# Layer a's reciprocals of the sums of weights: held in the buffer of their spread copies instead of the buffer of the FFN's normalized row

## The chip, the cores and the metric

The kernel runs on one core of one Trainium2 chip. The metric is the time of one execution on the device in microseconds (us), as the median of three runs. One more execution was taken with the hardware profiler, and all durations below come from that one.

## The reference, cut to what matters

The input `x` has 4 sequences of 2048 rows of 512 values in fp32. Four layers follow each other, each on a layer norm of the running `x` and each added to it: a linear attention with 16 heads of 64 (layer a), an FFN in int8, a gated recurrence (layer b), and the same FFN again. The change lies in layer a and its FFN:

```python
q = relu(q) + EPS;  k = relu(k) + EPS
k_cumsum = cumsum(k, axis=2)
context  = cumsum(einsum('bhnd,bhne->bhnde', k, v), axis=2)
D_inv = 1.0 / einsum('bhnd,bhnd->bhn', k_cumsum, q)      # reciprocal of the sum of weights
attn  = einsum('bhnd,bhnde,bhn->bhne', q, context, D_inv)
x = x + attn @ Wo + bo
# FFN: each row of layernorm(x) is divided by its largest magnitude / 127, rounded, and multiplied
x = x + ffn(layernorm(x), rhs)
```

## The kernel before, in words

**Tiles and stages.** The program has two bodies; the one that these inputs take is `layer_a_mild` followed by `layer_b_mild`. Layer a cuts the 8192 rows into 16 blocks of 512 (`n` = 0 to 15, four for each sequence) and the 16 heads into 8 pairs (`hp` = 0 to 7). For each block the loop goes over the pairs. I call one turn of it a pair step. In a pair step, `attend(B, hp)` gives the attention work of that pair in six parts (`keys`, `scores`, `update`, `weigh`, `outputs`, and an empty one), and `spread` puts the filler matmuls between them. The filler is: the keys and queries of the next pair (`feature`), a piece of the values (`values`), and the tail of the block before: in steps 0 to 3 the output projection of one row tile of 128 rows (`project`, tile `po`, line 648), in steps 4 to 7 the FFN product of one row tile (`pf`, line 681).

**One pair step, by engine.** TensorE forms `pk` and `pq`; VectorE turns them into `kT` and `qT` (line 804). A copy of `kT` is split into 16-bit `planes` (line 710), turned by a DMA transpose (line 712) and joined by ScalarE into `kr` (line 717). TensorE forms the scores `pss` (line 888), VectorE masks them into `sm` (line 894), one for each head. TensorE forms the updates `pu`, ScalarE copies them to `u` (line 909), and GpSimd adds them into `within` in three dependent rounds of two additions (line 914): the state in front of each of the four chunks. Then TensorE forms the outputs `pn` from these states (line 968) and from `sm` (line 974), ScalarE copies them to `oT` (line 983), and GpSimd makes the last addition into `state` (line 979). VectorE keeps running sums of the keys in `qc` (lines 869, 872, 876).

**The weights, every fourth pair.** In steps 3 and 7, `weigh` sums the weights of four pairs in `pd` (line 926). ScalarE takes the logarithm into `f_y` (line 931) and the exponential of its negative into `guess` (line 933), each with a table load ahead of it; VectorE improves this reciprocal by one Newton step (lines 935 and 936); a DMA stores eight rows of it to `rec` in DRAM (line 938), and pairs of DMAs read it back with each row copied over 64 partitions into `wide` (line 959), two pairs of heads at a time. `divide` multiplies `oT` by `wide` (line 950) in the pair step that follows. The tile `guess` carries the name `f_xn`.

**The FFN of the block before.** `levels(prev, i)` is written after pair steps 3 to 6 for row tiles 0 to 3: statistics (lines 124 to 127; 126 and 127 run on GpSimd), the normalized row in `f_xn` (line 131), its largest magnitude (664 to 666), the scaled and rounded row (668, 670) in `f_q`, and a DMA transpose into `f_qT` (line 676). In block 0 the same buffer `f_xn` also takes the four parts of the FFN's weight while they are quantized (line 691).

**What sets the order.** Tiles are named buffers of a pool; tiles with the same name share its `bufs` slots, and `f_xn`, `f_y` and `wide` have one slot each. A scheduler fixes the order of the instructions on each engine when the program is built, from the order of the code, the dependencies, and the moment at which a slot comes free. At run time every engine works its own list strictly in order. PSUM tiles of the tag `mm` (`pk`, `pq`, `pv`, `po`, `pf`, `pd`) share three banks in rotation.

Of the kernel before, what the change touches and what calls it, by code (L numbers as in the profile page):

```python
# [10 lines left out]
F32 = mybir.dt.float32  # L11
# [8 lines left out]
P = 128  # L20
# [9 lines left out]
TA = 512  # L30
# [16 lines left out]
def hybrid_block_kernel(ctx: ExitStack, tc: tile.TileContext, t: dict, out: bass.AP):  # L47
# [674 lines left out]
    def layer_a_mild():  # L722
        with ExitStack() as es:
            w = es.enter_context(tc.tile_pool(name="ma_w", bufs=1))
            pool = es.enter_context(tc.tile_pool(name="ma", bufs=2))
# [123 lines left out]
            def attend(B, hp):  # L849
# [69 lines left out]
                def weigh():  # L919


                    if hp % 4 != 3:
                        return
                    pd = bank([P, TA], F32, name="pd", tag="mm")
                    for m in range(4):
                        nc.tensor.matmul(
                            pd[m * 32 : (m + 1) * 32, :], same, B.qc[hp - 3 + m],
                            start=True, stop=True, skip_group_check=True,
                        )
                    ln = pool.tile([P, TA], F32, name="f_y", bufs=1)  # L930
                    nc.scalar.activation(ln, pd, AF.Ln)
                    guess = pool.tile([P, TA], F32, name="f_xn", bufs=1)
                    nc.scalar.activation(guess, ln, AF.Exp, scale=-1.0)

                    nc.vector.scalar_tensor_tensor(ln, pd, -1.0, guess, ALU.mult, ALU.mult)
                    nc.vector.scalar_tensor_tensor(guess, ln, 2.0, guess, ALU.add, ALU.mult)
                    rec = dram.tile([4, 2, TA], F32, name=f"rec_{B.n}_{hp}")
                    nc.sync.dma_start(rec.rearrange("m h t -> (m h) t"), guess[0:P:16, :])

                    if B.n + 1 == len(at) and hp == NP - 1:  # L940
                        wide = pool.tile([P, 4, TA], F32, name="xnTa")
                        for h, r in enumerate(heads):
                            nc.sync.dma_start(wide[r, :, :], rec[:, h, :].partition_broadcast(DA))
                        wides = [wide[:, 0:2, :], wide[:, 2:4, :]]
                    else:
                        wides = [load(rec, 0)]

                    def divide(m):
                        o = B.oT[hp - 3 + m]
                        nc.vector.tensor_tensor(o, o, wides[m // 2][:, m % 2, :], ALU.mult)  # L950
                        if m == 1 and len(wides) == 1:
                            wides.append(load(rec, 2))

                    weights.extend([lambda m=m: divide(m) for m in range(4)])

                def load(rec, m):
                    wide = pool.tile([P, 2, TA], F32, name="wide", bufs=1)
                    for h, r in enumerate(heads):
                        nc.sync.dma_start(wide[r, :, :], rec[m : m + 2, h, :].partition_broadcast(DA))
                    return wide  # L960

                def outputs():
# [20 lines left out]
                    nc.scalar.copy(B.oT[hp], pn.rearrange("p i t -> p (i t)"))  # L983

                return [keys, scores, update, weigh, outputs, lambda: None]

            def block(n, x):
# [574 lines left out]
```

## Time and profile before

| | |
|---|---|
| median of three runs | 4108.96 us (4106.58 to 4109.81) |
| profiled execution: its own time / its span | 4114.83 / 4113.0 us |
| TensorE busy | 3992.1 us, 97% of the span |
| VectorE / GpSimd / ScalarE busy | 57% / 36% / 21% of the span |
| mean granted TensorE clock | 0.989 |
| layer a | from 0 to about 2480 us; an inner block takes about 151 us |
| one pair step of an inner block | about 21.4 us in steps 0 to 2, about 15.4 us in steps 5 and 6 |

The profile was read in one execution. A wait of an engine is the idle time ahead of an instruction, put down to what ended it. Matmuls are pipelined and their ends are modelled, so a TensorE that looks busy may still not be at its peak; its idle stretches, on the other hand, are real.

### The profile page before, as it was taken

Reading aid. Unit: us, or ns where it says so; the run is one execution under the profiler, and the core shown is the slowest. Engines: PE = TensorE matmul, PEld = TensorE weight load, DVE = VectorE, ACT = ScalarE, POOL = GpSimd, SP = SyncE. Lnnn points to the kernel's source line nnn. Section 1 sums busy time; section 2 is a strip of 40 time slices with the busy share of each in tenths; the row PEclk is TensorE's granted clock in tenths of the full one; section 3 lists DMA queues with packets and bytes.
Section 4 is the critical chain, followed back from the end, with each engine's and each line's share of the span. In section 5 each row is a group of like instructions: output and inputs, shape, how many; then the busy total and the mean of one; then the engine's idle time right before and its main releaser. Section 6 shows DMA issues by size and latency. Waiting matters only on the chain.

```text
span 4113.0 us, 54684 instructions
## 1 busy us (share of the span) xinstructions
PE 3992.1 (97%) x21333; PEld 2203.9 (54%) x21333; DVE 2363.5 (57%) x4575; ACT 884.0 (21%) x1420; POOL 1492.9 (36%) x2527
## 2 busy tenths in 40 slices
PE   8999999999999999999999987999999999999997
PEld 4554554554544554554554544666666666666664
DVE  4455555555555455455455455666666666666665
ACT  2222212222222222222122111222222222222221
POOL 3122322322232323232232223455444554444543
PEclk9999999999999999999999998999999999999998
DMA  4112212212222222221121123121221221211111
GB/s 134 33 38 58 61 37 62 57 39 65 52 42 65 55 53 51 52 67 38 51 68 39 37 51 123 42 52 47 51 48 47 47 48 48 49 49 47 52 32 28
DMA packets 432045, 217.32 MB, mean 53 GB/s; under 512 B 363808, under 2 KB 376992, under 8 KB 431776
## 3 DMA queue, kind: packets, MB, share of 16 engines
q1 hardware_dynamic: 430656, 212.16, 21.3%
q8 instruction: 169, 2.77, 0.3%
q10 hardware_dynamic: 1120, 1.57, 0.1%
q14 instruction: 100, 0.82, 0.1%
HBM read 91.49 MB, written 34.08 MB: 31 GB/s over the span
## 4 chain that ended last, share of the span: by engine, by line
PE 72%; DVE 10%; POOL 10%; DMA 4%; issue 2%; ACT 2%; SPq 0%; POOLq 0%; DVEq 0%; ACTq 0%
PE pk L648 10%; PE pv L648 9%; PE pq L648 9%; PE pr L1215 8%; PE po L648 8%; PE py L648 5%; PE pvb L648 3%; PE pss L888 3%; PE pn L974 3%; PE pn L968 2%; PE pf L681 2%; DVE st L124 2%; PE ps L1308 2%; POOL rs L127 2%; PE pl L1248 2%
## 5 line engine op out<-in xcount | busy, mean ns | idle before, releaser
L648 PE MATMUL pq<-xnTa,a_Wq 128*128 128x512 f32 x1024 | 493.6, 610 | 0.0
L648 PE MATMUL pk<-xnTa,a_Wk 128*128 128x512 f32 x1024 | 491.1, 604 | 0.0
L648 PE MATMUL pv<-a_Wv,xnTa 128*128 128x512 f32 x1024 | 477.3, 605 | 2.9 <-ACT xnTa L141 2.9
L648 PE MATMUL po<-a_Wo_sb,oT 128*128 128x512 f32 x1024 | 468.7, 603 | 7.0 <-DVE oT L950 6.9
L914 POOL TENSOR_TENSOR within<-state,u 64x64 f32<-64x64 f32 x256 | 129.9, 507 | 654.7 <-ACT u L909 645.1
L126 POOL TENSOR_SCALAR rs<-mv 128x1 f32<-128x1 f32 x320 | 85.8, 269 | 728.1 <-DVE mv L125 530.7
L648 PEld LDWEIGHTS po<-a_Wo_sb,oT 128*128 128x128 f32 x1024 | 189.7, 191 | 236.7 <-issue 217.7
L648 PEld LDWEIGHTS pv<-a_Wv,xnTa 128*128 128x128 f32 x1024 | 189.5, 192 | 234.8 <-issue 229.9
L909 ACT COPY u<-pu 128x256 f32<-128x256 f32 x128 | 47.6, 372 | 1131.3 <-PE pu L904 1036.3
L648 PEld LDWEIGHTS pq<-xnTa,a_Wq 128*128 128x128 f32 x1024 | 182.2, 190 | 193.6 <-issue 183.3
L648 PEld LDWEIGHTS pk<-xnTa,a_Wk 128*128 128x128 f32 x1024 | 184.8, 190 | 180.6 <-issue 157.7
L894 DVE TENSOR_TENSOR sm<-pss,causal 128x512 f32<-128x512 f32 x256 | 164.7, 685 | 193.0 <-PE pss L888 193.0
L1215 PE MATMUL pr<-xnTb,m_kT_sb 128*128 128x256 f32 x1024 | 259.5, 392 | 0.0
L1215 PE MATMUL pr<-xnTb,m_qT_sb 128*128 128x256 f32 x1024 | 253.4, 391 | 0.0
L648 PE MATMUL pvb<-b_vT_sb,xnTb 128*128 128x512 f32 x512 | 242.7, 607 | 0.0
L648 PE MATMUL py<-b_oT_sb,yT 128*128 128x512 f32 x512 | 231.6, 594 | 0.0
L838 DVE TENSOR_TENSOR xa<-po,xa 128x512 f32<-128x512 f32 x64 | 44.1, 690 | 320.3 <-PE po L648 320.3
L1215 PEld LDWEIGHTS pr<-xnTb,m_qT_sb 128*128 128x128 f32 x1024 | 188.1, 191 | 63.7 <-issue 31.5
L1354 POOL TENSOR_TENSOR state_b<-pairs,m_diag 128x256 f32<-128x256 f32 x128 | 98.4, 769 | 327.9 <-DVE pairs L1332 298.1
L1215 PEld LDWEIGHTS pr<-xnTb,m_kT_sb 128*128 128x128 f32 x1024 | 184.7, 190 | 51.0 <-issue 19.9
L914 POOL TENSOR_TENSOR within<-within,u 64x64 f32<-64x64 f32 x512 | 192.2, 375 | 38.4
L717 ACT COPY kr<-turned 128x1024 uint16<-128x1024 uint16 x120 | 139.3, 1160 | 302.3 <-DMA turned<-planes 302.3
(157 smaller groups left out, 6533.2 us busy)
## 6 DMA issues: line engine op xcount, KB each, us to landing
wide<-rec SPq DMA_DIRECT2D x124, 256.0 KB, 3.6
mmid<-xa SPq DMA_DIRECT2D x16, 1024.0 KB
out<-xb SPq DMA_DIRECT2D x32, 512.0 KB, 2.8
xa<-in_x SPq DMA_DIRECT2D x15, 1024.0 KB
xb<-mmid SPq DMA_DIRECT2D x30, 512.0 KB, 7.4
turned<-planes SPq DMA_TRANSPOSE x304, 3.1
m_cos<-in_cos SPq DMA_DIRECT2D x30, 128.0 KB, 2.4
m_sin<-in_sin SPq DMA_DIRECT2D x30, 128.0 KB
```

Source lines behind the costliest of these rows:

```text
L124: nc.vector.bn_stats(st[:, i, :], x[:, i, :])
L126: nc.gpsimd.tensor_scalar(rs, mv[:, :, 1], LN_EPS, None, ALU.add)
L127: nc.gpsimd.tensor_tensor(rs, rs, neg_half[:, :n], ALU.pow)
L648: nc.tensor.matmul(held[0], lhs(), rhs(), start=(n == 0), stop=(n == len(pairs) - 1))
L681: nc.tensor.matmul(pf, qT[:, c, :], rq[:, c, :], start=(c == 0), stop=(c == KC - 1))
L717: nc.scalar.copy(dst.bitcast(U16).rearrange("p n (t two) -> p n t two", two=2), turned.rearrange("p (two n) t -> p n t two", two=2),)
L888: nc.tensor.matmul(ps[h][:, i, :], k[r, chunks[i]], q[r, chunks[i]], start=True, stop=True)
L894: nc.vector.tensor_tensor(s, ps[h], causal.unsqueeze(1).to_broadcast([P, NTA, P]), ALU.mult)
L914: nc.gpsimd.tensor_tensor(A.before[i + 1][r, r], A.before[i][r, r], u[r, i, :], ALU.add)
L974: nc.tensor.matmul(pn[r, i, :], v()[:, i, vh[h]], A.sm[h][:, i, :], start=False, stop=True, skip_group_check=True,)
L1215: nc.tensor.matmul(pr[:, half, :], wp[name][:, c, lo : lo + P], B.xnT[:, c, :], start=(c == 0), stop=(c == KC - 1),)
L1354: nc.gpsimd.tensor_tensor(st.rearrange("p (q c) -> p q c", c=2 * DB), pairs[:, g, :].unsqueeze(1).to_broadcast([P, HG // 2, 2 * DB]), smal ...
```

## The change

The tile that holds `guess` takes the name `wide` instead of `f_xn`. It is the first half of a tile of the shape that `load` uses, so that it lives in the one slot of `wide`. No arithmetic, no transfer and no buffer is added or removed.

```diff
                     ln = pool.tile([P, TA], F32, name="f_y", bufs=1)
                     nc.scalar.activation(ln, pd, AF.Ln)
-                    guess = pool.tile([P, TA], F32, name="f_xn", bufs=1)
+                    guess = pool.tile([P, 2, TA], F32, name="wide", bufs=1)[:, 0, :]
                     nc.scalar.activation(guess, ln, AF.Exp, scale=-1.0)
 
                     nc.vector.scalar_tensor_tensor(ln, pd, -1.0, guess, ALU.mult, ALU.mult)
                     nc.vector.scalar_tensor_tensor(guess, ln, 2.0, guess, ALU.add, ALU.mult)
                     rec = dram.tile([4, 2, TA], F32, name=f"rec_{B.n}_{hp}")
                     nc.sync.dma_start(rec.rearrange("m h t -> (m h) t"), guess[0:P:16, :])
```

## The prediction

> **What bounds the kernel now.** I first read the busy shares, then what TensorE waits for, then the timeline of one inner block of layer a on all engines.
>
> ```profile
> PE 3992.1 (97%) x21333; PEld 2203.9 (54%) x21333; DVE 2363.5 (57%) x4575; ACT 884.0 (21%) x1420; POOL 1492.9 (36%) x2527
> PE pf L681 <- DMA f_qT<-f_q: 25.4, 5, 9.1
> PE pn L968 <- POOL within L914: 21.1, 25, 1.2
> ```
>
> TensorE sets the end: 97% busy, so only its own idle time can be won, and a VectorE wait costs something only if TensorE later runs dry. Its waits (sum, times, longest) show where. `pf` on `f_qT` falls on the last microseconds of layer a and on layer b, outside the change. The 25 waits on `within` are layer a's. By the timeline 1.82 us of them fall in block 0 and 1.21 in steps 5 and 6 of block 15; the other 18.04 us all stand in pair step 4: in blocks 1 to 14 they are 1.21, 0.81, 2.17, 0.81, 0.83, 0.83, 1.55, 0.90, 0.81, 0.80, 0.83, 0.81, 0.82, 2.13 (sum 15.31), in block 15 0.77 + 0.96 + 1.00 = 2.73. Block 4 stands for the others (start, duration, engine, ...; in brackets the idle time before it):
>
> ```profile
> 706.17 0.63 ACT L933 ACTIVATE f_xn<-f_y 128x512 f32<-128x512 f32 x1
> 710.38 0.55 DVE L131 TENSOR_SCALAR f_xn<-xa,mv,rs 128x512 f32<-128x512 f32 x1 [1.63 <-DMA rec<-f_xn]
> ...
> 719.05 1.28 DVE L894 TENSOR_TENSOR sm<-pss,causal 128x512 f32<-128x512 f32 x2
> ...
> 722.69 1.54 DVE L950 TENSOR_TENSOR oT<-oT,wide 128x512 f32<-128x512 f32 x2
> 724.15 1.34 DVE L869 TENSOR_TENSOR_SCAN qc<-go,kT 128x512 f32<-128x512 f32 x1
> ...
> 721.76 1.19 POOL L914 TENSOR_TENSOR within<-state,u 64x64 f32<-64x64 f32 x2
> 723.02 3.07 POOL L914 TENSOR_TENSOR within<-within,u 64x64 f32<-64x64 f32 x4
> ...
> 726.15 0.49 PE L968 MATMUL pn<-qT,within 128*128 128x128 f32 x2 [0.81 <-POOL within L914]
> ```
>
> VectorE has no gap from 710.38 to 730.2, because all four FFN rows are packed behind the store of `guess`. The last four GpSimd additions take 3.07 us there; in step 0 of the same block they take
>
> ```profile
> 657.14 0.70 POOL L914 TENSOR_TENSOR within<-state,u 64x64 f32<-64x64 f32 x2 [3.69 <-ACT u L909]
> 657.91 1.48 POOL L914 TENSOR_TENSOR within<-within,u 64x64 f32<-64x64 f32 x4
> ```
>
> They are slow while VectorE runs lines 950 and 869, so the third pair of `pn` matmuls starts at 726.15 instead of 725.34.
>
> [...] 3.07 against 1.48 us under lines 950 and 869 (two SBUF inputs each), and in step 5 the first two additions take 1.61 instead of 0.70 under line 869. [...]
>
> **The change, part by part.** The lists of instructions of the changed program, which has not run, show what moves.
>
> (1) Removed: the FFN rows no longer wait for `guess` to be stored. That wait is 27.0 us of VectorE in 15 times, none of it on TensorE: worth 0 by itself.
>
> (2) Added: `guess` waits for the slot of `wide`. The last `divide` is at 724.2 in step 4, the next `guess` at 773.6 in step 7, the one after in the next block: free some 50 us ahead, 0. The other way, `wide` cannot be loaded before `guess` is stored, but the load reads `rec`, so it waits for that store already: 0. Nothing queued on SP sees a new wait from it.
>
> (3) Moved: rows 0, 1 and 2 go on VectorE to steps 0, 1 and 2, right behind line 838 and the statistics, ahead of `sm`; row 3 stays in step 4. GpSimd's lines 126 and 127 for rows 0 to 2 go along, at 0.22 + 0.57 us each, while GpSimd is idle. Two `f_qT` transposes (1.2 us of SP each) go to steps 0 and 1, ahead of that step's `turned`; `f_q` is done just before `planes`, so `kr` slips by at most one transpose more.
>
> What it costs in steps 0 to 2: from the trace of step 4 one row takes 2.67 us (710.38 to 713.05), after 1.05 us for the two GpSimd instructions. In step 2, line 838 starts at 692.31, statistics end at 693.93, the row runs from 694.98 to 697.65, so `sm` comes at 697.65 instead of 695.97 and `planes` 1.7 us later than 697.89. TensorE needs `sm` at 707.6 and the bank of `pk` at 705.7: covered. In steps 0 and 1 `sm` comes 2.5 us later; line 869 then falls on the third round of `within` (658.8 to 660.1), which ends near 660.4 instead of 659.4, while TensorE asks for it at 663.3 in step 0: 2.9 us of cover. So 0.
>
> What it brings in step 4: the later `planes` of step 2 delays `kr`, and on ScalarE `kr` stands ahead of the logarithm.
>
> ```profile
> 701.79 1.16 ACT L717 COPY kr<-turned 128x1024 uint16<-128x1024 uint16 x1 [1.97 <-DMA turned<-planes]
> 702.97 1.28 ACT L931 ACT_TABLE_LOAD   x1
> 782.60 1.29 DVE L950 TENSOR_TENSOR oT<-oT,wide 128x512 f32<-128x512 f32 x2 [3.18 <-DMA wide<-rec]
> ```
>
> So line 936 ends at 708.49 + 1.66 = 710.15. Store and spread take 6.3 us (step 7: line 936 ends at 776.26, line 950 starts at 782.60). VectorE is idle in between, line 950 starts at 716.45, and the list goes on: 838, 950, statistics to 719.13, row 3 starts at 720.2, its line 664 ends at 721.4, `sm` to 722.6, `kT` 723.4, `planes` 724.2. Only then, 724.2 to 726.7, come line 869 and two of line 950. `u` is ready at 721.5; six additions of 0.37 us with their gaps, from 721.76, end near 724.1, ahead of the 725.34 that TensorE needs. I leave 0.1 us a block for chance overlap. In block 15, counted the same way (`u` 0.25 us behind TensorE), 0.25 us remains. The late `qT` (728.7) still frees its bank before 730.3.
>
> Gain: 18.04 - 14 x 0.1 - 0.25 = 16.4 us.
>
> (4) Block 0: `guess` waited for the quantized part in `f_xn` and held ScalarE until 111.9, with `rscale` behind it, for which TensorE waited 0.51 us. That wait goes; two instead of four score matmuls stand ahead of the transpose, so I count 0.3 us.
>
> Sum: -16.7 us. The profiled execution took 4114.83 us, of which 1.83 lie around its span; it becomes 4098.1. The median lies 5.9 us below that execution, so 4108.96 - 16.7 = **4092.3 us**, -0.41%. Unknown: [...] the landing of `wide` in its new surroundings (6.3 us, perhaps 1 either way).
>
> **Rivals.** I take 0.2% of the time, 8.2 us, as what a measurement of this kernel can tell from no change.
>
> A. *The blocked stretch only shifts.* If `kr` is not delayed by all of 1.7 us, line 869 starts near 723.3, and the last two additions are caught behind it and line 950. The wait then stays at 0.7 to 0.8 us in every block: 14 x 0.75 = 10.5 of 15.31 remain, and about 1 us is won in block 15: 4108.96 - 5.8 = 4103 us. For it speaks that only 0.1 to 0.9 us separate the additions' end from line 869; against it, that each step of the delay is a direct wait in the trace.
>
> B. *Slower: `within` becomes late in steps 0 and 1.* Row, `sm`, `kT`, `planes` and 869 now run without a gap just when `within` is due. If the third round is held until line 876 is through as well (662.7), and the row starts later because its statistics stand second on GpSimd, it misses 663.3 by about 0.9 us in both steps: 2 x 15 x 0.9 = 27 us, less 16.7: 4119 us. It decides from 2.9 us of further delay on. The step is 21.4 us long, which speaks against it.
>
> C. *The 27 us of VectorE wait come off the end*: 4082 us. TensorE shows no gap at those times, so hardly.
>
> D. *The change does nothing* (the slot of `wide` is busy, the rows wait as before): 4109 us; the lists already show the rows moved, so only as part of "same".
>
> **How the numbers follow.** My forecast 0.58, A 0.25 (a little of it beyond 8.2 us), B 0.12, C 0.02, D 0.03. Faster by over 0.2%: 0.58 + 0.02 + 0.05 of A = 0.65. Same: 0.20 + 0.03 = 0.23. Slower: 0.12. The forecast's own range is 4088 (all of 21.1 us but block 0's, and some noise) to 4100. For eight in ten it reaches over A: 4086 to 4108.
>
> **What would show it.** Right: the waits of `pn` on `within` fall from 21.1 us to about 4.7; in step 4 the last four additions take about 1.5 us; the wait on `rec` is gone from `f_xn`; `f_xn` rows stand in steps 0 to 2; the exponential of step 3 comes 1.7 us later against TensorE. Wrong: waits of `pn` of 0.7 us still in step 4 (A), new waits in steps 0 and 1 (B), or a new wait of TensorE on `kT`, `qT` or `sm`.

## The result, and the profile after

The changed kernel takes **4083.38 us** (median of four runs, 4082.97 to 4084.23) against 4109.09 us before (4106.58 to 4109.81) in the same comparison: ratio 0.9939, 95% interval 0.9922 to 0.9956. That is 25.7 us less. The prediction said 4092.3 us, with 4086 to 4108 as its range: the direction was right, the gain half as large again as forecast. The profiled execution took 4082.97 us, its span 4081.2 us. Two executions in a slow state, of 8099.94 us (late1) and 5806.78 us (one_input), are left out of the medians given below.

Busy shares, and TensorE's waits (sum, times, longest), of the changed kernel:

```profile
PE 3972.0 (97%) x21211; PEld 2197.0 (54%) x21333; DVE 2356.3 (58%) x4575; ACT 875.9 (21%) x1420; POOL 1506.4 (37%) x2527
```
```profile
PE pf L681 <- DMA f_qT<-f_q: 24.9, 5, 9.1
PE po L648 <- DVE oT L950: 6.1, 2, 5.7
PE pn L968 <- POOL within L914: 4.1, 7, 1.2
```

The busy shares say nothing here (122 matmul records are missing from this trace). The waits do: those of `pn` on `within` went from 21.1 us to 4.1, where 4.7 was forecast. That is 17.0 us, and the kernel became 25.7 us faster. The rest of this text is about that difference.

Timeline of block 4, pair step 4, of the changed kernel, on ScalarE, VectorE, GpSimd and TensorE:

```profile
714.25 0.37 ACT L909 COPY u<-pu 128x256 f32<-128x256 f32 x1 [10.74 <-PE pu L904]
```
```profile
709.58 0.69 DVE L950 TENSOR_TENSOR oT<-oT,wide 128x512 f32<-128x512 f32 x1 [6.23 <-DMA wide<-rec]
...
713.36 0.55 DVE L131 TENSOR_SCALAR f_xn<-xa,mv,rs 128x512 f32<-128x512 f32 x1 [1.07 <-POOL rs L127]
...
716.51 0.69 DVE L710 COPY planes<-kT 128x1024 uint16<-128x1024 uint16 x1
717.12 1.34 DVE L869 TENSOR_TENSOR_SCAN qc<-go,kT 128x512 f32<-128x512 f32 x1
718.39 1.47 DVE L950 TENSOR_TENSOR oT<-oT,wide 128x512 f32<-128x512 f32 x2
```
```profile
714.70 0.70 POOL L914 TENSOR_TENSOR within<-state,u 64x64 f32<-64x64 f32 x2 [1.38 <-ACT u L909]
715.48 1.90 POOL L914 TENSOR_TENSOR within<-within,u 64x64 f32<-64x64 f32 x4
```
```profile
717.84 0.83 PE L968 MATMUL pn<-qT,within 128*128 128x128 f32 x6
```

I measure from the start of the `u` copy (line 909), because TensorE sets it in both kernels. The additions end at 715.48 + 1.90 = 717.38, which is u + 3.13; before it was 723.02 + 3.07 - 721.14 = u + 4.95. Line 869 starts at u + 2.87 and the last two of line 950 behind it, so that they hardly touch the additions (the last four take 1.90 us, against 1.48 in step 0 of block 4 before). All six `pn` matmuls run in one stretch of 0.83 us.

**Where the time came from.** The distance from one `u` copy to the next gives the length of a step without any model of where a matmul ends. From the copy of step 4 to that of step 5, blocks 1 to 14 take 14.51 to 14.57 us now. Before, ten of them took 15.59 to 15.73 us (I call these ten the plain blocks), block 1 16.21, block 7 16.64, block 3 18.76, block 14 18.83; block 15 went from 17.35 to 11.68. The sum over the 15 blocks falls by 28.8 us, of the 31.8 us by which the two spans differ; the waits listed there had been 18.04 us. Outside block 0 the other steps have kept their lengths within 0.1 us, but for the stretch from step 0 to step 1, where 2.2 us of scattered waits are gone.

### The profile page after: what moved, and what is told of

Same layout as the page of the kernel before. It is cut to its first block, busy times and chain, and to the rows that moved or that the text cites. A ratio compares the mean times of both kernels' runs of the same rounds, so it can differ in the third digit from the quotient of the medians.

```text
span 4081.2 us, 54608 instructions
## 1 busy us (share of the span) xinstructions
PE 3972.0 (97%) x21211; PEld 2197.0 (54%) x21333; DVE 2356.3 (58%) x4575; ACT 875.9 (21%) x1420; POOL 1506.4 (37%) x2527
## 4 chain that ended last, share of the span: by engine, by line
PE 83%; POOL 8%; DVE 6%; issue 1%; DMA 1%; ACT 0%; SPq 0%; POOLq 0%; ACTq 0%; DVEq 0%
PE pk L648 11%; PE pv L648 11%; PE pq L648 11%; PE po L648 11%; PE pr L1215 8%; PE py L648 5%; PE pss L888 3%; PE pvb L648 3%; PE pn L974 3%; PE pn L968 3%; PE pf L681 2%; PE pu L904 2%; PE ps L1308 2%; PE pl L1248 2%; PE pg L648 2%; DVE st L124 2%
## 5 line engine op out<-in xcount | busy, mean ns | idle before, releaser
L126 POOL TENSOR_SCALAR rs<-mv 128x1 f32<-128x1 f32 x320 | 70.7, 221 | 765.9 <-DVE mv L125 765.6
L914 POOL TENSOR_TENSOR within<-state,u 64x64 f32<-64x64 f32 x256 | 156.5, 611 | 523.0 <-ACT u L909 513.4
L127 POOL TENSOR_TENSOR rs<-rs,neg_half 128x1 f32<-128x1 f32 x320 | 193.4, 605 | 23.3
```

The costliest lines, as they stand in the source:

```text
L127: nc.gpsimd.tensor_tensor(rs, rs, neg_half[:, :n], ALU.pow)
L914: nc.gpsimd.tensor_tensor(A.before[i + 1][r, r], A.before[i][r, r], u[r, i, :], ALU.add)
```

## The experiments

Two questions: why does step 4 become faster, and why by more than its waits? *Theory M*: VectorE instructions that read two tiles (lines 950 and 869) no longer run on top of GpSimd's additions. *Rival S*: the 27 us that the FFN rows waited for a store were the cost. On the price: a *linear* price (a wait costs its idle time) against *theory P* (more). The answers in short: the wait for the store cost almost nothing by its length, but it set the order of VectorE's work so that lines 950 and 869 fell on the additions; and a wait of TensorE cost more than its idle time, by a lost overlap of matmuls (0.27 us in a plain block) and, where waits piled up, by the clock (0.50 for 3.41 us or more). In the expectations, "the sum of the waits" is that of the profile's list. Each comparison had its own runs of the kernel before, with medians of 4111.3 to 4112.5 us.

### What a wait costs: late1, late2, late4

The changed kernel, with one, two or four useless GpSimd instructions that make `within` late.

```diff
                     nc.scalar.copy(u, pu)
+                    if B.n and hp == 4:
+                        for _ in range(2):      # 1, 2, 4
+                            nc.gpsimd.tensor_scalar(u, u, 1.0, None, ALU.mult)
```

> The changed kernel with two multiplications by 1 of `u` on GpSimd ahead of the additions in step 4 of blocks 1 to 15: `within` comes some 0.8 us later there. It measures what a wait of TensorE costs. In the changed kernel the additions end 0.3 to 0.9 us before TensorE needs them, so a wait of 0 to 0.5 us in each of 15 blocks. Linear price (a wait costs its idle time): lost time = sum of the new waits, 0 to 8 us. Theory P (a wait costs its idle time and about 0.27 us more for the restart of the matmuls, and far more where two waits stand close): 1.3 to 1.6 times the sum of the waits.

> As with two multiplications, but four: `within` some 1.6 us later, waits of 0.7 to 1.5 us in each of 15 blocks, some in two or three pieces. Linear price: lost time = sum of the new waits, 10 to 22 us. Theory P: each wait costs about 0.27 us more than its idle time, and where two or three of them stand within 3 us the granted clock falls behind them and the price is about 2 us for each us of idle time: lost 20 to 40 us, and the intervals between the `u` copies of these steps lengthen by more than the waits listed in them.

> The changed kernel with one multiplication by 1 of `u` on GpSimd ahead of the additions in step 4 of blocks 1 to 15. With two of them the waits were 33 us longer and the time 68 us. Linear price: lost time equals the new waits. Theory P: where one wait stands alone, the step lengthens by its idle time and 0.2 to 0.3 us more, at a full granted clock; where two or three stand within 3 us, by twice the idle time, at a clock of 0.5 to 0.9 over some 4 to 8 us. Waits of 0.3 to 0.8 us, in one piece in most blocks: 4095 to 4105 us.

Medians: 4102.70 us with one, 4151.69 with two, 4194.01 with four; that is 19.3, 68.3 and 110.6 us above the changed kernel. The waits of `pn` (one line each from the profiles of late1, late2 and late4):

```profile
PE pn L970 <- POOL within L916: 18.6, 23, 1.2
```
```profile
PE pn L971 <- POOL within L917: 37.5, 45, 1.4
```
```profile
PE pn L971 <- POOL within L917: 61.4, 49, 4.2
```

Over the 4.1 us of the changed kernel these are 14.5, 33.4 and 57.3 us more. A microsecond of listed wait costs 1.3, 2.0 and 1.9 us. The linear price is refuted. The waits were longer than I had expected (in block 4 a useless instruction takes 0.86 to 1.36 us, at least twice what I had assumed). The price for single waits was as expected in late1, where most blocks have one wait of 1.02 to 1.15 us and a step 1.2 to 1.4 us longer; for piled waits it was the 2 that I had expected of late4, and it was that in late2 already, where I had expected 1.3 to 1.6.

**The first part of the price** is lateness that is not shown as idle. One plain block (block 4) in each kernel, both times measured from its own `u` copy:

| kernel | additions end | wait listed | step longer than 14.57 |
|---|---|---|---|
| changed | 3.13 | 0 | 0 |
| one_input_869 | 3.65 | 0 | 0 |
| kr_pe | 4.03 | 0 | 0.15 |
| one_input | 4.42 | 0.28 | 0.54 |
| before | 4.95 | 0.81 | 1.08 |
| rows_stored | 4.98 | 0.57 | 1.10 |
| late1 | 5.17 | 1.02 | 1.26 |

The last column is the first minus 3.9, within 0.03 us, in all rows where it is above zero. So TensorE is held up from u + 3.9 on, not from u + 4.2 as the prediction took from the waits. Before, four `pn` matmuls took 0.61 us and the last two, behind the wait, 0.49 us; without the wait all six take 0.83. The overlap of matmuls that follow each other was lost at the wait, and that 0.27 us (0.61 + 0.49 - 0.83) appears as busy time. In rows_stored it was lost twice: its first four `pn` matmuls on `within` take 0.88 us, with no wait listed among them.

**The second part** is the clock. TensorE in late2, block 4, and four windows of the same step (us, busy time of PE, PEld, DVE, ACT and POOL, granted TensorE clock, DMA share, GB/s):

```profile
728.16 0.49 PE L971 MATMUL pn<-qT,within 128*128 128x128 f32 x2 [0.56 <-POOL within L917]
729.61 0.49 PE L971 MATMUL pn<-qT,within 128*128 128x128 f32 x2 [0.96 <-POOL within L917]
730.67 0.79 PE L971 MATMUL pn<-qT,within 128*128 128x128 f32 x2 [0.57 <-POOL within L917]
731.39 1.98 PE L977 MATMUL pn<-sm,va 128*64 128x128 f32 x16
```
```profile
723.90:727.90 4.00, 3.70 (x10) 1.59 (x9) 4.00 (x8) 0.32 (x1) 3.35 (x4) 1.00 0.20 67
727.90:731.90 4.00, 2.20 (x12) 1.60 (x14) 3.97 (x10) 1.16 (x1) 3.47 (x7) 0.83 0.34 66
731.90:735.90 4.00, 4.00 (x20) 2.36 (x18) 0.86 (x4) 1.24 (x2) 0.18 (x1) 0.74 0.35 68
735.90:739.90 4.00, 4.00 (x26) 2.05 (x24) 0.75 (x1) 1.09 (x2) 1.26 (x1) 1.00 0.16 33
```

After three short waits (2.09 us of idle time within 3 us) the clock falls to 0.74 over four microseconds. The 16 matmuls on `sm` take 1.98 us instead of 1.09 while no engine keeps them waiting. The additions end at u + 6.77, so the rule of the table gives 2.9 us; the step is 4.37 us longer. The kernel before did the same in blocks 3 and 14. Its TensorE and its windows in block 3:

```profile
572.46 0.49 PE L968 MATMUL pn<-qT,within 128*128 128x128 f32 x2 [0.96 <-POOL within L914]
574.15 0.80 PE L968 MATMUL pn<-qT,within 128*128 128x128 f32 x2 [1.21 <-POOL within L914]
574.88 1.98 PE L974 MATMUL pn<-sm,va 128*64 128x128 f32 x16
```
```profile
571.50:575.50 4.00, 1.83 (x10) 1.42 (x12) 4.00 (x7) 1.16 (x1) 3.00 (x6) 0.82 0.34 66
575.50:579.50 4.00, 4.00 (x20) 2.32 (x17) 2.62 (x9) 0.61 (x2) 0.18 (x1) 0.76 0.42 68
```

The additions end at u + 6.57 there: 2.7 us by the rule, 4.2 measured. The excess comes in steps. In late2 it is 0 in block 1 (waits 1.43 + 0.83), 1.6 us in block 6 (1.41 + 0.83), 2.9 us in block 5 (1.43 + 0.83). The granted clock gives the size of these steps: from 60 to 2480 us of every trace, which is nearly all of layer a, it is either 1.00 or lowered to 0.50 for 3.41 us or a whole multiple of it. Half the clock for 3.41 us loses 1.7 us of work (an estimate from these two numbers); the traces show 1.5 to 1.7, or about twice that. The starts in one execution lie whole multiples of 3.413 us apart (in late2 at 576.96, 730.56, 884.16 and 1041.18 us: 45, 45 and 46 of them); I call the stretches of 3.413 us on this grid its windows. The clock fell without a window that is idle throughout: no wait in step 4 of late2 is longer than 1.43 us. The falls go with how much idle time lies in one window of this grid. Two windows each of before_again and before_again2 (two more executions of the kernel before) show it in block 7, where the waits are 0.64 + 1.21 and 0.62 + 1.21 us:

```profile
1178.75:1182.17 3.42, 1.62 (x18) 1.31 (x19) 3.42 (x7) 1.16 (x1) 2.71 (x5) 1.00 0.40 77
1182.17:1185.58 3.41, 3.41 (x12) 1.53 (x9) 2.82 (x10) 0.59 (x1) 0.18 (x1) 0.50 0.40 77
```
```profile
1180.28:1183.70 3.42, 2.21 (x21) 1.62 (x21) 3.42 (x8) 1.75 (x2) 1.78 (x4) 1.00 0.14 25
1183.70:1187.11 3.41, 3.41 (x11) 1.50 (x11) 2.18 (x8) 0.65 (x1) 0.18 (x1) 1.00 0.40 77
```

In before_again nearly all of both waits falls into one window, in which TensorE is busy for 1.62 us, and the next window runs at half clock. In before_again2 the grid cuts between the waits, TensorE is busy for 2.21 us of the second window, and nothing is lost. In that stretch of all sixteen traces, every fall follows a window with 1.43 us or more of idle time (2.06, 2.12 and 1.74 us in blocks 3, 14 and 15 of the kernel before); of the windows at full clock that no fall followed, only two had more than 1.45 us (1.62 and 1.87, in late4; 1.21 is the most in the kernel before). The loss doubled where the first slow window had 0.16 us or more of idle time itself, for then the next was slow too (1.00 us in block 15 of the kernel before, where the clock stood at 0.50 for 6.83 us); behind one with 0.11 us or less (0.11 and 0.00 in its blocks 3 and 14) the clock rose. All these idle times rest on the modelled ends of the matmuls.

### What stretches the additions: one_input, one_input_869, one_input_all

The kernel before, its wait for the store and its order on all engines kept; only the VectorE instructions on top of the additions read one tile instead of two.

```diff
-                        nc.vector.tensor_tensor(o, o, wides[m // 2][:, m % 2, :], ALU.mult)
+                        if B.n and hp == 3 and m >= 2:
+                            nc.vector.tensor_scalar(o, o, wides[m // 2][:, m % 2, 0:1], None, ALU.mult)
+                        else:
+                            nc.vector.tensor_tensor(o, o, wides[m // 2][:, m % 2, :], ALU.mult)
...
-                    nc.vector.tensor_tensor_scan(qc, go, k, 0.0, ALU.mult, ALU.add)
+                    if B.n and hp == 5:         # one_input_869; hp == 4 in one_input_all
+                        nc.vector.tensor_scalar(qc, k, go[:, 1:2], None, ALU.mult)
+                    else:
+                        nc.vector.tensor_tensor_scan(qc, go, k, 0.0, ALU.mult, ALU.add)
```

> The kernel before, in which the last two of line 950 in step 4 of blocks 1 to 15 multiply `oT` by the first column of `wide` (one operand for each partition) instead of by the whole tile, so that they read one tile instead of two; all else, the order on every engine too, is as before (the weights of heads pairs 2 and 3 are so left out, but for one column). The FFN rows keep their wait for the store to `rec`, and VectorE is as late as before. Theory M (the additions are held up by VectorE instructions that read two tiles): the four last additions take 1.5 to 2.2 us instead of 3.07, the waits of `pn` on `within` in step 4 fall to under 4 us, time 4083 to 4092 us. Rival S (the wait for the store is the cost): no change, 4107 to 4112 us.

> As with one operand for each partition in the last two of line 950, and line 869 of step 4 in blocks 1 to 15 likewise (a copy of `kT` in place of its running sum), so that no VectorE instruction on top of the additions reads two tiles; the order on GpSimd, TensorE, ScalarE and SP is as before the change, and the FFN rows keep their wait for the store (the weights of three pairs are so left out or changed). With line 950 alone the step took 15.09 us in plain blocks, 15.62 before, 14.55 in the changed kernel. Theory M: the additions end before TensorE needs them, the step takes 14.55 us in nearly every block, 4083 to 4090 us. If something else in the kernel before costs time as well (the later start of the additions behind line 127, the wait for the store): the step stays at 14.8 to 15.1 us, 4093 to 4103 us.

> The kernel before, with the last two of line 950 in step 4 of blocks 1 to 15 on one operand for each partition, and the line 869 that runs right behind them (that of pair 5) likewise, a copy of `kT` in place of its running sum; the order on every engine is as before the change (the weights of three pairs are so left out or changed). Theory M: the last four additions take 1.5 to 1.9 us instead of 2.54, they end 3.4 to 3.8 us after `u`, the step takes 14.55 us in plain blocks (1, 3, 7, 14 and 15 start their additions later and keep some wait), 4088 to 4097 us. If something else stretches the additions: 15.05 us and 4102 us as without this edit.

With line 950 alone: 4102.23 us (ratio 0.9976, 0.9965 to 0.9987), the last four additions 2.54 us, the step 15.06 to 15.11 us in nine plain blocks and 15.29 in block 8. That is half of the effect on a plain block's step; less than expected, and more than rival S allows. one_input_all missed its target: the line 869 that runs behind `u` of step 4 belongs to pair 5, and I had changed that of pair 4, which runs in step 3. So it repeats one_input (4102.41 us, step 15.06 to 15.14 us, 14.98 in block 8). one_input_869 changes the right one: 4093.04 us (0.9949, 0.9933 to 0.9966). GpSimd in its block 4:

```profile
718.58 1.18 POOL L917 TENSOR_TENSOR within<-state,u 64x64 f32<-64x64 f32 x2
719.84 1.77 POOL L917 TENSOR_TENSOR within<-within,u 64x64 f32<-64x64 f32 x4
```

3.07 us have become 2.54 and then 1.77, and the step takes 14.51 to 14.57 us in all ten plain blocks, the length of the changed kernel. In these blocks nothing but the collision cost time. The substitutes are shorter as well (0.54 us each, instead of 0.80 and 1.34), but this doesn't explain it: in block 4 the four additions run on top of them in 0.38 to 0.39 us each, where under the two-tile instructions they had taken 0.43 to 1.12. The waits of the FFN rows for the store are still there, from its view of VectorE's waits:

```profile
DVE f_xn L131 <- DMA rec<-f_xn: 27.3, 15, 3.6
```

Blocks 1, 3, 7, 14 and 15 start their additions 1.4 to 2.6 us after `u` in this kernel, others 0.6; they keep 7.9 us. The kernel before has the same five. Its VectorE and GpSimd in block 3 (`u` at 567.53):

```profile
558.38 0.55 DVE L131 TENSOR_SCALAR f_xn<-xa,mv,rs 128x512 f32<-128x512 f32 x1 [3.25 <-DMA rec<-f_xn]
```
```profile
568.64 0.51 POOL L126 TENSOR_SCALAR rs<-mv 128x1 f32<-128x1 f32 x1 [14.52 <-DVE f_sc L666]
569.23 0.85 POOL L127 TENSOR_TENSOR rs<-rs,neg_half 128x1 f32<-128x1 f32 x1
569.76 1.18 POOL L914 TENSOR_TENSOR within<-state,u 64x64 f32<-64x64 f32 x2
```

`u` is ready at 567.9, but GpSimd has the statistics of an FFN row ahead of the additions, and these wait for VectorE. In block 3 the store took VectorE 3.25 us instead of 1.62, and the additions start 1.6 us later than in block 4; in block 7 it was 2.62, and they start 1.0 us later. In these two blocks of all five traces that keep this order (the kernel before three times, one_input, one_input_869) the two delays agree within 0.01 us. That is a second way from the store's wait to TensorE, beside the collision. In blocks 1, 14 and 15 the store's wait is 1.6 us as elsewhere, but the exponential itself was 0.7, 1.7 and 0.8 us later against `u` than in block 4. In blocks 1 and 14 ScalarE had waited 2.66 and 3.62 us, instead of 1.97, for the transpose of `kr` ahead of the logarithm; in block 15 the step before is 0.85 us shorter. Why these transposes and stores landed late stays open. In the changed kernel the statistics are through before `u`, and the additions start at u + 0.45 in all 15 blocks.

### What keeps lines 950 and 869 away: in_y, rows_held, rows_stored

All three are shown against the changed kernel.

```diff
# in_y: neither in f_xn
-                    ln = pool.tile([P, TA], F32, name="f_y", bufs=1)
+                    ln = pool.tile([P, 2, TA], F32, name="wide", bufs=1)[:, 0, :]
-                    guess = pool.tile([P, 2, TA], F32, name="wide", bufs=1)[:, 0, :]
+                    guess = pool.tile([P, TA], F32, name="f_y", bufs=1)
# rows_held: the slot of f_xn is held until line 936 is through
+                    hold = pool.tile([P, D], F32, name="f_xn", bufs=1)
+                    nc.vector.tensor_copy(hold[:, 0:1], guess[:, 0:1])
# rows_stored: and until it is stored
+                    rec1 = dram.tile([8, 1], F32, name=f"rec1_{B.n}_{hp}")
+                    nc.sync.dma_start(rec1, hold[0:P:16, 0:1])
```

> The logarithm takes the slot of `wide` and `guess` that of `f_y`, so neither of them uses `f_xn`. Theory M (what matters is that the FFN rows may leave step 4, because `f_xn` is free early): as fast as the changed kernel, 4083 us within 3, with no more than 5 us of waits of `pn` on `within`. Rival W (the gain needs `guess` itself in the slot of `wide`, through the order in which `wide` is stored and loaded): 4095 us or more.

> `guess` stays in the slot of `wide`, but a copy of one column after line 936 holds `f_xn` until then, so that the FFN rows 0 to 2 stay packed behind line 936, without a wait for the store to `rec`. Theory M: most of the gain is lost, since the rows again fill VectorE ahead of `sm` and lines 950 and 869: 4098 to 4110 us, with `pn` waiting on `within` in step 4 again (10 us or more in all). Rival S (the 27 us that VectorE waited for the store to `rec` were what cost the time): 4083 us, since that wait is gone here as well.

> The changed kernel, with one column of `guess` copied to a tile named `f_xn` and stored in DRAM: the FFN rows wait for a store again, as before the change, though `guess` stays in the slot of `wide`. The order of VectorE in step 4 is not quite that of before: the third row is through ahead of `sm`, and line 869 stands ahead of the last two of line 950. Rival S (the wait of the rows for a store is the cost, 1.6 us in each block): 4105 to 4112 us. Theory M (only lines 950 and 869 on top of the additions cost): they come later here, at the end of the additions or behind it: under 6 us of waits of `pn` on `within`, 4083 to 4093 us.

in_y: 4082.01 us (0.9930, 0.9913 to 0.9946), 1.4 us from the changed kernel: what counts is that `f_xn` is free, and rival W is out. rows_held: 4087.47 us. Theory M had expected 4098 to 4110 and was wrong as I had put it; rival S, with 4083, was nearer. The rows stand packed behind line 936 again, and the exponential starts 14.95 us ahead of `u` as before the change (13.39 in the changed kernel; medians of the 15 blocks); yet step 4 takes 14.51 to 14.57 us in blocks 1 to 14, and its sum is 28.4 us below that of the kernel before. So taking away the wait for the store is enough for nearly all of the 28.8 us; neither the move of the rows nor the later exponential is needed. (Its 4 us over the changed kernel lie between steps 0 and 1.) rows_stored: 4103.41 us. Here the number speaks for rival S, and my expectation of theory M failed too; VectorE of block 4 shows why (`u` at 714.88):

```profile
704.64 0.55 DVE L131 TENSOR_SCALAR f_xn<-xa,mv,rs 128x512 f32<-128x512 f32 x1 [2.09 <-DMA rec<-f_xn]
...
715.89 1.34 DVE L869 TENSOR_TENSOR_SCAN qc<-go,kT 128x512 f32<-128x512 f32 x1
717.15 1.47 DVE L954 TENSOR_TENSOR oT<-oT,wide 128x512 f32<-128x512 f32 x2
```

Line 869 starts at u + 1.0 and both of line 950 follow, all on top of the additions, which end at u + 4.98. In rows_held these lines start at u + 2.9. The wait for the store makes them *earlier*: two rows instead of three are finished ahead of the first line 950, so that the third row fills the place in which VectorE otherwise waits 1.07 us for the statistics of the fourth (the bracket at line 131 of the changed kernel, above). In plain blocks, then, the wait costs time through the order of the rows and the collision, not by its length: one_input_869 keeps it whole and loses nothing there.

### Is the prediction's chain needed: kr_pe, kr_pe4, no_newton

```diff
# kr_pe: pair 3; kr_pe4: pair 4 (in two places)
-                    if name == "k" and B.n:
+                    if name == "k" and B.n and hp != 3:
# no_newton
+                    if not (B.n and hp == 3):
                         nc.vector.scalar_tensor_tensor(ln, pd, -1.0, guess, ALU.mult, ALU.mult)
                         nc.vector.scalar_tensor_tensor(guess, ln, 2.0, guess, ALU.add, ALU.mult)
```

> The changed kernel, with the keys of step 3 turned by TensorE instead of the DMA and ScalarE, so that line 931 has no `kr` ahead of it; TensorE has about 0.6 us more work in each of 15 blocks (9 us). The prediction's chain (later `kr`, later exponential, later `wide`, later line 869) is needed: without it line 869 starts 1.3 to 1.6 us earlier against `u`, on top of the additions, and `pn` waits 0.5 to 0.8 us in step 4 in most blocks: 4105 us or more. It is not needed: no such waits, some 4092 us.

> The changed kernel, with the keys of pair 4 turned by TensorE in blocks 1 to 15, so that no `kr` stands ahead of the logarithm; TensorE has 0.44 us more in each block (6.6 us), as the earlier kernel with pair 3 showed. If the prediction's chain (later `kr`, later exponential, later `wide`) is needed: the exponential comes 1 us or more earlier against `u`, lines 950 and 869 fall on the additions, and the step lengthens by 0.5 to 1.1 us in most blocks: 4097 to 4108 us. If only the absence of the FFN rows counts: no such lengthening, 4089 to 4093 us.

> The changed kernel without the Newton step (lines 935 and 936) in step 3 of blocks 1 to 15: `wide` is stored and loaded some 1.5 us earlier, about what the later `kr` had delayed it by; the FFN rows 0 to 2 stay in steps 0 to 2 (the weights of these pairs are a little less exact). If the prediction's chain decides (the later exponential keeps lines 950 and 869 off the additions): they fall on top of them again, the step lengthens to 15.0 to 15.6 us in most blocks, 4090 to 4100 us. If the rows' absence alone decides: the step stays at 14.55 us, 4080 to 4085 us.

kr_pe, 4091.60 us, missed its target as one_input_all did: the `kr` ahead of the logarithm is that of pair 4. Its 6.6 us more of TensorE work are seen (the stretch from the `u` copy of step 2 to that of step 3 is 0.44 us longer in each block), and no wait came back. kr_pe4: 4098.94 us (0.9966, 0.9952 to 0.9980). Of the 15.6 us over the changed kernel, 6.6 are TensorE's work and 6.2 are step 4, which lengthens by 0.75 to 0.95 us in six blocks and 1.0 in block 15; in the others the additions end at u + 3.80 to 3.94, just in time. Another 1.5 us lie between steps 0 and 1. no_newton: 4090.45 us (0.9953, 0.9936 to 0.9970); in the profiled execution (4087.36 us) two blocks lose 0.96 and 1.12 us, block 15 0.68, the others up to 0.29. In both, the order of VectorE's list around `sm` differs a little as well. So the later logarithm is a part of the cause, which decides in some of the blocks once the rows have moved; most of the gain comes without it, and in rows_held nearly all.

### The kernel before, twice more: before_again, before_again2

> The kernel before once more. In its first profiled execution (4114.83 us) five blocks had two or three waits of `pn` close together in step 4, or one at a later round, and these blocks alone lost about 11 us more than a plain block does. If the scatter of the kernel before (4106 to 4115 us) comes from how many blocks do so, an execution of another time has another number of them, and the sum of the step 4 intervals differs by as much as the time does. If it comes from elsewhere, the sum of these intervals stays within 1 us.

> The kernel before a third time, with the same two expectations: the sum of the step 4 intervals follows the time of the execution, or it stays within 1 us.

Profiled executions of 4114.79 and 4113.61 us. Their step 4 sums are 242.6 and 242.4 us, against 244.1 in the first (4114.83). The single blocks differ: block 7 took 18.59 and 16.93 us, after waits of 0.64 + 1.21 and 0.62 + 1.21 us. So the slow clock came and went with waits that differ by 0.02 us, as the windows shown above explain. All three profiled executions lie above the medians of the kernel before (4109 to 4112); why stays open, and their times are too close together to tell what its scatter comes from.

## Why the prediction was right or wrong

- **(1) The FFN rows' wait for the store is worth 0 by itself.** Its length is worth nothing in plain blocks, as one_input_869 shows; but it also sets the order of VectorE's work, and that the prediction left out. rows_held takes away the wait and leaves the rows and the exponential where they were, and step 4 becomes 28.4 us shorter; rows_stored brings it back and loses 20 us against the changed kernel. In blocks 3 and 7 even its length counts: what is above 1.6 us of it came through to TensorE by the statistics on GpSimd.
- **(2) The new waits for `wide` cost 0.** Right: `po` on `oT` went from 6.9 to 6.1 us.
- **(3) Rows in steps 0 to 2 cost 0.** Right: these steps keep their length; rival B is out. The exponential came 1.59 us later against `u` (forecast 1.66), line 869 at u + 2.87 (forecast u + 3.06), the additions ended at u + 3.13 (forecast u + 2.96), and TensorE has no wait left in step 4 but 0.29 us in block 15 (forecast 0.25). Rival A is out; the 0.1 us a block for chance overlap were not needed. So the chain came about as forecast, but as a cause the moved rows and the later exponential were overstated, as kr_pe4, no_newton and above all rows_held show.
- **The step that failed: the 18.04 us of waits, counted one to one.** Step 4 became 28.8 us shorter. Blocks 1 to 14 had 15.31 us of waits and gained 23.1: the additions' lateness (against u + 3.88, the value of the table before rounding) makes 19.9, and the slow clock in blocks 3 and 14 makes 3.1. Block 15, with three waits in a row, gained 5.7 where 2.5 was counted; there the clock had stood at one half from 2386.52 to 2393.34 us. The lower end of the range, "all of 21.1 us but block 0's", rested on the same count, and therefore did not hold.
- **(4) Block 0: 0.3 us gained.** Wrong by 0.8: `rscale`'s wait is gone and that step is 0.57 us shorter, but the next has a wait on `within` of 0.76 and is 1.06 us longer.
- **The sum on the median.** The profiled execution of before lay 5.7 us above its median. The two profiled executions differ by 31.9 us, where 16.7 was forecast: 12.4 us more in step 4, 2.2 from step 0 to step 1, 1.3 behind the last `u` copy, and 0.8 less in block 0. The medians differ by 25.7; so 6.2 us of what the two traces show are not in the medians, since the trace of before was slower than its usual.
- **Rival C** named nearly the right time (4082 us) by another way, that the 27 us come off the end one to one. They don't: in one_input_869 the same wait stands beside 14.54 us steps.

## What to carry to other kernels

Price a TensorE wait by how late its operand is against the moment at which the matmul would have started in an unbroken stream, and look at the granted clock behind places where several waits come close: here the list of waits showed three quarters of the loss for single waits and half of it for piled ones. Where GpSimd is on the path of TensorE, keep VectorE instructions that read two tiles, as lines 950 and 869 do, off the stretch in which it works: in block 4 its last four additions took 3.07 us under these two, 1.77 under their one-tile substitutes in one_input_869, and 1.48 in step 0, where neither falls on them. What moves them there may be a buffer's name several steps away. Before an experiment removes an instruction, read from the trace which pair or block it belongs to: two of mine changed its neighbour.

## What I had not expected of the hardware

- In block 3 of the kernel before, two waits of 0.96 and 1.21 us within 3 us were enough to take the granted clock to one half for 3.41 us, with 1.5 us lost; 2.06 us of idle time lay in one window of the clock's grid. In block 7, waits of 0.62 + 1.21 us brought no fall in before_again2, where 0.64 + 1.21 us did in before_again.
- The additions were stretched in plain blocks even where VectorE's instruction reads one tile: the first two took 1.18 instead of 0.70 us under lines 670 and 710 in one_input_869. Under that kernel's one-tile substitutes for lines 950 and 869 the last four took 0.38 to 0.39 us each; what sets these apart from lines 670 and 710, no run here shows.
